# End of the second layer's attention: scores of a step ahead of its product with v, and the last FFN's first weights loaded into attention's weight tiles

## The chip, the cores and the metric

The kernel runs on one core of one Trainium2 chip. The time is that of one execution in device microseconds (us). A run repeats the execution; the median of three runs of the kernel before is 3238.61 us (3231.18 to 3245.23). One further execution was profiled: it took 3235.61 us, its instructions span 3233.8 us, and the granted TensorE clock was 0.990 of full speed on average.

The engines are called as the profile calls them: PE is TensorE (matmuls), PEld its weight loads, DVE is VectorE, ACT is ScalarE, POOL is GpSimd, SP issues DMAs.

## The reference

Two layers, each `x = x + attention(norm(x)) * silu(ffn(norm(x)))`, on x of 4 x 1024 x 512 in fp32. The change concerns the second layer, from the end of its attention on:

```python
# attention of layer 1: 16 heads of 32, rotary positions, softmax over 1024 keys
q, k, v = proj(wq), proj(wk), proj(wv)
q, k = apply_rope(q, k, sin, cos)
att = softmax(einsum('bhqd,bhkd->bhqk', q, k) / sqrt(32))
y = einsum('bhqk,bhkd->bhqd', att, v)
s = y.reshape(b, t, c) @ wo.T

# FFN of layer 1: weights are int32, DIM = 512, HID = 1408
def _qlinear(x, wq, scale):
    W = (wq.astype(float32) - 128.0) * scale[:, None]
    return einsum('bsd,hd->bsh', x, W)
g = silu(_qlinear(silu(_qlinear(x, wq_gate, s_gate)) * _qlinear(x, wq_up, s_up), wq_down, s_down))
x = x + s * g
```

## The kernel before

The kernel has four stages, one after the other: attention and FFN of layer 0 (to about 1200 us of the span), attention of layer 1 (1200 to 2714 us) and FFN of layer 1 (2714 us to the end). On PE the order of instructions is the order in which the program gives them. On the other engines and on SP's DMA queue a scheduler sets the order when the kernel is built, unless an instruction is kept in program order. Every queue is worked off strictly in its order. Tiles come from pools by a tag; a tag with `bufs` buffers hands them out in turn, and a new tile waits until the readers of the tile that had the buffer are done.

**Attention of layer 1** (L702 to L1018) works in 32 units: a batch, a group of four heads and a half of the 1024 queries each. Keys are cut into 8 blocks of 128. The main loop (L933) makes one step `s` after the other. In step `s` the unit's scores are first computed for their maxima alone (`top`, L863: PE into two PSUM tiles `sq`, DVE reduces each, L876). After 8 steps `turn_max` (L878) transposes the maxima; ACT copies them twice and DVE forms `mT` (L888). Ten steps behind (`LAG`), step `e = s - 10` computes its scores again, transposed, with the maxima subtracted by a second matmul (`expo`, L892: tiles `sk`, matmuls L899 and L905), and ACT takes the exponential of the two halves (L910) into `pT`, which has three buffers. `weigh` (L914) multiplies the `pT` of step `e - 1` with v into `y`. POOL sums the `pT` of a unit's 8 steps into `part` (L1013, L1015), and `total` (L809) sums `part` over the keys with a matmul by ones. For the last unit there is no `part`: PE sums each of its 8 `pT` (`z_last`). `divide` (L817) copies the sums (ACT), inverts them in four pieces (DVE, L825) and scales y (POOL, L826) to `yT`. `sq` and `sk` share three PSUM tiles (`ring`).

Within a step the order on PE is: `sq`, then `weigh` of `e - 1`, then a piece of other work (projections of the next heads, or the output projection `wo_out`, L829), then `expo` of `e`, then more of the other work. After step 255 there are no maxima left and, but for the sums, no other work: steps 256 to 266 only run `weigh` and `expo`. Then eight chains of the output projection follow, four for each half of the last batch's queries, each with an ACT copy and a DMA of its result.

**FFN of layer 1** (`ffn1_slots`, L1026) opens its pools when those of attention are closed. It loads 33 integer weight tiles (11 each of gate, up and down, 256 KB) through four staging buffers `wint`; DVE subtracts 128 (`weight`, L1050, L1058). The activations of a block of 512 tokens come in four pieces and are split into two parts, by ACT and DVE (`prep2`, L1032 to L1046). Per slot a gate and an up chain of eight matmuls each are made, and up to four pairs of matmuls for the down product of earlier slots (`down`, L1102). `gate` (L1112) makes the output of a tile of 128 tokens: DVE, ACT (L1121), DVE, DVE, POOL (L1124), DMA out, with two buffers for each of its four tiles. DVE also takes each weight tile's greatest magnitude (`most`, L1146), which decides at the end whether a second path has to run; the program places these from slot 22 on.

Of the kernel before, what the change touches and what calls it, by code (L numbers as in the profile page):

```python
# [12 lines left out]
F32 = mybir.dt.float32  # L13
# [22 lines left out]
def kernel(ctx, tc, ins, out):  # L36
# [634 lines left out]
    s1_t = s1.rearrange("(t p) d -> t p d", p=P)  # L671
    with ExitStack() as es:
# [3 lines left out]

        w0 = es.enter_context(tc.tile_pool(name="a1w", bufs=1, reuse_waits="tile"))
# [244 lines left out]

        es.enter_context(tc.manual_schedule(engines={mybir.EngineType.PE}))
# [9 lines left out]
        for s in range(TB * nu + LAG + 1):  # L933
# [27 lines left out]
            if s < TB * nu:  # L961
                u, j = divmod(s, TB)
                if j == 0:
                    mx[u] = p2.tile([P, TPB, 4, 2], F32, tag="mx", name=f"mx_{u}")
                for pair in range(2):
                    top(u, j, pair, mx[u])
                if j == TB - 1:
                    m2 = twice[u % 2].rearrange("p q (h c) -> p q h c", c=HD)
                    for c in range(2):
                        nc.vector.tensor_reduce(m2[:, :, :, c], mx[u], AX.X, ALU.max, negate=True)  # L970
                    del mx[u]
            if 1 <= e <= TB * nu:
                u, kb = divmod(e - 1, TB)
                if kb == 0:
                    ys[u] = pp.tile([P, 512], F32, tag="y", name=f"y_{u}")
                weigh(u, kb, pTs[e - 1], ys[u])
                if u == nu - 1:

                    if kb == 0:
                        z_last = acc1("z_last")  # L980
                    total(z_last, pTs[e - 1], kb, TB)
                pTs.pop(e - 2, None)
                if kb == TB - 1:
                    yr = p2.tile([P, 512], F32, tag="yr", name=f"yr_{u}", bufs=1)
                    nc.scalar.copy(yr, ys[u])
                    ys[u] = yr
                    if u == nu - 1:
                        divide(units[u], yr, z_last)
            held = 0
            if s % TB == 0 and 0 < s <= TB * nu:  # L990
                turn_max(s // TB - 1)
            elif s % TB == 4 and 0 <= s // TB - 2 < nu - 1:
                u = s // TB - 2
                z = ring(f"z_{u}")[:, 0, :] if s >= TB * nu else acc1(f"z_{u}")
                total(z, parts.pop(u), 0, 1)
                divide(units[u], ys.pop(u), z)
                b, g, qh = units[u]
                if g == 3:
                    soon[s + 4] = b, qh, yTs[b]
            elif s in lates:  # L1000
                late_turn(*lates.pop(s))
            else:
                held = 1
                advance(1)
            if 0 <= e < TB * nu:
                u, kb = divmod(e, TB)
                pT = pTs[e] = p2.tile([P, 4, 512], F32, tag="pT", name=f"pT_{e}", bufs=3)
                expo(u, kb, pT)
                if u == nu - 1:
                    pass  # L1010
                elif kb == 1:
                    parts[u] = p2.tile([P, 4, 512], F32, tag="part", name=f"part_{u}")
                    nc.gpsimd.tensor_tensor(parts[u], pTs[e - 1], pT, ALU.add)  # L1013
                elif kb:
                    nc.gpsimd.tensor_tensor(parts[u], parts[u], pT, ALU.add)  # L1015
            advance(4 - held)
        for new in [*soon.values(), (*units[-1][::2], yTs[B - 1])]:
            spare.extend(wo_out(*new, spread))  # L1018
        for chain in spare:
            advance(8)  # L1020
# [5 lines left out]
    def ffn1_slots():  # L1026
# [8 lines left out]
        def prep2(blk):  # L1035

            b, h = divmod(blk, 2)
            xs = p2.tile([P, KD, BLK], F32, tag="xs", name=f"xs_{blk}", bufs=1)
            xp = [a.bitcast(F32R) for a in xpair(f"xp1_{blk}")]
            for k in range(KD):  # L1040
                nc.sync.dma_start(out=xs[:, k, :], in_=xnT_d[b][k, :, h * BLK : (h + 1) * BLK])
                nc.scalar.copy(xp[0][:, k, :], xs[:, k, :])
                nc.vector.tensor_tensor(
                    xp[1][:, k, :], xs[:, k, :], xp[0][:, k, :].bitcast(F32), ALU.subtract
                )
            return xp  # L1046

        ws = {}

        def weight(n, c):  # L1050
            q = p2.tile([P, KD, P], I32, tag="wint", name=f"{n}_int{c}", bufs=4)
            if n == "down":
                src = ins["wq_downT"][c * P : (c + 1) * P, :].rearrange("p (k n) -> p k n", n=P)
            else:
                src = ins[f"wq_{n}T"][:, c * P : (c + 1) * P].rearrange("(k p) n -> p k n", p=P)
            nc.sync.dma_start(out=q, in_=src)
            w = ws[n, c] = wp.tile([P, KD, P], F32R, tag=f"{n}{c}", name=f"w{n}{c}")
            nc.vector.tensor_scalar(w, q, -128.0, None, ALU.add)  # L1058

        xp = prep2(0)  # L1060
        sg = wp.tile([P, NH1], F32, tag="sg", name="sg")
        nc.sync.dma_start(out=sg, in_=ins["s_gate"])
        su = wp.tile([P, NH1], F32, tag="su", name="su")
        nc.sync.dma_start(out=su, in_=ins["s_up"])
        for c in range(NH1 + 2):
            for n, d in (("gate", c), ("up", c), ("down", c - 2)):
                if 0 <= d < NH1:
                    weight(n, d)
        sdb = wp.tile([P, D], F32, tag="sdb", name="sdb")
        nc.sync.dma_start(out=sdb, in_=ins["s_down"].partition_broadcast(P))  # L1070

        sg2 = wp.tile([P, NH1], F32, tag="sg2", name="sg2")
        nc.vector.tensor_scalar(sg2, sg, 0.5, None, ALU.mult)
        sgu = wp.tile([P, NH1], F32, tag="sgu", name="sgu")
        nc.vector.tensor_tensor(sgu, sg2, su, ALU.mult)

# [35 lines left out]
        def gate(blk, i):  # L1112
            t = blk * TPB + i
            s = p2.tile([P, D], F32, tag="s", name=f"s1_{t}")
            nc.sync.dma_start(out=s, in_=s1_t[t])
            x = p2.tile([P, D], F32, tag="x", name=f"x2_{t}")
            nc.sync.dma_start(out=x, in_=x1_t[t])
            z = p2.tile([P, D], F32, tag="z", name=f"z1_{t}")
            nc.vector.tensor_tensor(z, ds.pop(i), sdb, ALU.mult)
            th = p2.tile([P, D], F32, tag="th", name=f"th1_{t}")  # L1120
            nc.scalar.activation(th, z, AF.Tanh, scale=0.5)  # L1121
            nc.vector.scalar_tensor_tensor(th, th, 1.0, z, ALU.add, ALU.mult)
            nc.vector.scalar_tensor_tensor(th, th, 0.5, s, ALU.mult, ALU.mult)  # L1123
            nc.gpsimd.tensor_tensor(th, th, x, ALU.add)  # L1124
            nc.sync.dma_start(out=out_t[t], in_=th)
# [3 lines left out]
        for g in range(NH1 * NBLK + 2 + 2 * TPB):  # L1129
            blk, c = divmod(g, NH1)  # L1130
            if blk < NBLK:
                gated(blk, c, xp)
                if c == 5 and blk + 1 < NBLK:
                    nxt = prep2(blk + 1)
# [10 lines left out]
            if 0 <= m < len(order):  # L1145
                nc.vector.tensor_reduce(  # L1146
                    most[:, m : m + 1], ws[order[m]].bitcast(F32), AX.XY, ALU.max,
                    apply_absolute_value=True,
# [118 lines left out]
    with ExitStack() as es1:  # L1267
# [78 lines left out]
```

## Time and profile before

| what | value |
|---|---|
| median of three runs | 3238.61 us |
| the profiled execution, its own time | 3235.61 us |
| its span, first to last instruction | 3233.8 us |
| PE busy in the span | 3116.0 us, 96% |
| DVE, ACT, POOL busy | 58%, 37%, 47% |
| share of PE in the chain that ended last | 80% |
| attention's last step with maxima has its scores | 2631.1 us |
| last matmul of the last output chain of attention | 2714.5 us |
| first matmul of the last FFN | 2723.2 us |
| last matmul of the last FFN | 3220.2 us |

PE is busy for 96% of the span on average, so time can be won only where it waits, and lost wherever it is made to wait. An average hides where that is: it is read from windows of 10 us and from the chain of waits, which follows the work that ended last back from instruction to instruction. A busy PE is also not always a fast one, because its clock is lowered at times; the windows show the granted clock beside the busy time.

### The profile page before, as it was taken

The numbers are of one execution on the slowest core, as the hardware profiler recorded it, in microseconds if no ns is written. First come the engines' busy times: TensorE is split into PE (matmuls) and PEld (weight loads), VectorE is DVE, ScalarE is ACT, GpSimd is POOL, SyncE is SP. The second block draws the span as 40 slices with busy tenths as digits, with TensorE's granted clock in tenths as the row PEclk, the third lists the DMA queues.
The fourth block names the chain that finished last, engine by engine and source line by source line (L and its number), as shares of the span: only waits on it lengthen the run. The fifth ranks groups of instructions, "written<-read, shape, count | busy, mean of one in ns | idle before, by whom it ended". The sixth has DMA issues, their size and how long they took to land.

```text
span 3233.8 us, 61080 instructions
## 1 busy us (share of the span) xinstructions
PE 3116.0 (96%) x26221; PEld 1764.0 (55%) x26221; DVE 1876.7 (58%) x2670; ACT 1195.7 (37%) x1692; POOL 1510.1 (47%) x618
## 2 busy tenths in 40 slices
PE   8999999999999998999999999999999988999998
PEld 4555455577777764343344444433444325788886
DVE  6434743368888775556655655555555643755554
ACT  2111111055556542444444444444444442233222
POOL 0000000024444343898888888888988860000001
PEclk9999999999999999999999999999999999999999
DMA  5100300022222231100001000100000004222212
GB/s 190 55 27 27 103 29 14 24 69 78 89 79 69 92 131 51 37 8 8 8 17 39 13 10 13 41 15 15 11 15 14 11 1 138 96 74 66 69 49 66
DMA packets 96503, 158.46 MB, mean 49 GB/s; under 512 B 12896, under 2 KB 26464, under 8 KB 96096
## 3 DMA queue, kind: packets, MB, share of 16 engines
q1 hardware_dynamic: 95408, 151.33, 14.9%
q8 instruction: 207, 3.39, 0.4%
q0 software_dynamic: 816, 3.15, 0.3%
q14 instruction: 72, 0.59, 0.1%
HBM read 104.10 MB, written 41.94 MB: 45 GB/s over the span
## 4 chain that ended last, share of the span: by engine, by line
PE 80%; DVE 11%; DMA 4%; ACT 2%; issue 2%; SPq 1%; POOL 0%; POOLq 0%; ACTq 0%; DVEq 0%
PE sk L899 9%; PE sq L872 8%; PE y L918 8%; PE qk L318 6%; PE dn L1107 5%; PE up L1085 5%; PE gate L1085 5%; PE v1ps L730 4%; PE pj L571 3%; PE fc L518 3%; PE wo L730 3%; PE wk L730 3%; PE wq L730 3%; PE v0ps L292 3%; PE wo L301 3%; PE sk L905 2%
## 5 line engine op out<-in xcount | busy, mean ns | idle before, releaser
L1015 POOL TENSOR_TENSOR part<-part,pT 128x2048 f32<-128x2048 f32 x186 | 854.3, 4593 | 19.7 <-ACT pT L910 10.3
L876 DVE TENSOR_REDUCE mx<-sq 128x2 f32<-128x1024 f32 x512 | 603.4, 1217 | 403.7 <-PE sq L872 402.5
L910 ACT ACTIVATE pT<-sk 128x1024 f32<-128x1024 f32 x512 | 496.4, 1022 | 631.2 <-PE sk L905 629.0
L899 PE MATMUL sk<-wqT,wkT 32*128 32x512 f32 x2048 | 327.5, 643 | 4.5 <-DVE mx L876 4.5
L872 PE MATMUL sq<-wkT,wqT 32*128 32x512 f32 x2048 | 323.6, 643 | 8.1 <-ACT pT L910 6.3
L918 PE MATMUL y<-pT,v 128*32 128x512 f32 x2048 | 284.4, 608 | 12.8 <-ACT pT L910 12.8
L571 PE MATMUL pj<-wpj,hp 128*128 128x512 f32 x1024 | 265.2, 397 | 16.6 <-DVE hp L531 16.2
L1124 POOL TENSOR_TENSOR th<-th,x 128x512 f32<-128x512 f32 x32 | 41.4, 1293 | 494.6 <-DVE th L1123 393.8
L539 POOL TENSOR_TENSOR sums<-sums,h 128x512 f32<-128x512 f32 x112 | 163.5, 1460 | 226.4 <-ACT h L523 223.4
L518 PE MATMUL fc<-xp,wfc 128*128 128x512 f32 x1024 | 262.2, 398 | 2.3 <-ACT h L523 1.7
L905 PE MATMUL sk<-mT,onesr 2*128 2x512 f32 x1024 | 237.1, 789 | 0.0
L318 PE MATMUL qk<-xnT,wqkv 128*128 128x512 f32 x512 | 231.7, 606 | 3.2 <-DVE s L306 2.4
L571 PEld LDWEIGHTS pj<-wpj,hp 128*128 128x128 f32 x1024 | 189.8, 188 | 69.4 <-DVE hp L531 27.7
L325 POOL TENSOR_TENSOR qd<-qT,wqkv 128x512 f32<-128x512 f32 x32 | 41.2, 1289 | 389.7 <-ACT qT L323 362.9
L518 PEld LDWEIGHTS fc<-xp,wfc 128*128 128x128 f32 x1024 | 188.7, 189 | 42.9 <-ACT h L523 3.3
L1085 PE MATMUL gate<-xp,wgate 128*128 128x512 f32 x704 | 180.1, 398 | 8.8 <-DVE wgate L1058 8.8
L1085 PE MATMUL up<-xp,wup 128*128 128x512 f32 x704 | 179.0, 396 | 1.6 <-DVE h L1092 1.6
L1013 POOL TENSOR_TENSOR part<-pT,pT 128x2048 f32<-128x2048 f32 x31 | 141.3, 4557 | 80.8 <-ACT pT L910 80.7
L1107 PE MATMUL dn<-wdown,hp 128*128 128x512 f32 x704 | 177.8, 394 | 0.0
L899 PEld LDWEIGHTS sk<-wqT,wkT 32*128 32x128 f32 x2048 | 97.3, 183 | 136.7 <-issue 114.6
L531 DVE TENSOR_TENSOR hp<-h,hp 128x512 fp32r<-128x512 f32 x128 | 119.9, 936 | 84.6 <-ACT hp L528 84.6
L918 PEld LDWEIGHTS y<-pT,v 128*32 128x32 f32 x2048 | 41.8, 108 | 216.4 <-issue 188.2
(203 smaller groups left out, 4570.2 us busy)
## 6 DMA issues: line engine op xcount, KB each, us to landing
s<-s SPq DMA_DIRECT2D x96, 256.0 KB
x<-x SPq DMA_DIRECT2D x36, 256.0 KB
x<-in_x SPq DMA_DIRECT2D x32, 256.0 KB
raw_fc<-in_w_fcT SPq DMA_DIRECT2D x32, 256.0 KB
raw_pj<-in_w_projT SPq DMA_DIRECT2D x32, 256.0 KB
x0f<-in_x SPq DMA_DIRECT2D x32, 256.0 KB
x0r<-in_x SPq DMA_DIRECT2D x32, 256.0 KB
x<-th SPq DMA_DIRECT2D x32, 256.0 KB
```

Source lines behind the costliest of these rows:

```text
L318: nc.tensor.matmul(a, lhsT=wqkv[k][:, c0 : c0 + P], rhs=xnTs[blk][:, k, :], start=(k == 0), stop=(k == KD - 1),)
L518: nc.tensor.matmul(a, lhsT=wfc[k][:, c * P : (c + 1) * P], rhs=xp[n][:, k, :].bitcast(F32R), start=(k == 0 and n == 0), stop=(k == KD - 1 ...
L571: nc.tensor.matmul(ds[i], lhsT=hparts[blk, c][n][:, i * P : (i + 1) * P], rhs=wpj[c], start=(c == 0 and n == 0), stop=(c == NH0 - 1 and n ...
L730: nc.tensor.matmul(out[r0 : r0 + HD, :], lhsT=lhsT[:, r0 : r0 + HD], rhs=rhs, start=start, stop=stop,)
L872: nc.tensor.matmul(sq[:, hh, :], lhsT=qT[r, q0 : q0 + P], rhs=kT[r, n * 512 : (n + 1) * 512], start=True, stop=True,)
L876: nc.vector.tensor_reduce(mx[:, qt, 2 * pair : 2 * pair + 2, n], sq, AX.X, ALU.max)
L899: nc.tensor.matmul(sks[h // 2][:, h % 2, :], lhsT=kT[r, kb * P : (kb + 1) * P], rhs=qT[r, qh * 512 : (qh + 1) * 512], start=True, stop=False,)
L910: nc.scalar.activation(pT[:, 2 * pair : 2 * pair + 2, :], sks[pair], AF.Exp, scale=QKS)
L918: nc.tensor.matmul(y[r, :], lhsT=v[:, kb, r], rhs=pT[:, h, :], start=(kb == 0), stop=(kb == TB - 1),)
L1015: nc.gpsimd.tensor_tensor(parts[u], parts[u], pT, ALU.add)
L1085: nc.tensor.matmul(a, lhsT=ws[n, c][:, k, :], rhs=xp[m][:, k, :], start=(k == 0 and m == 0), stop=(k == KD - 1 and m == 1),)
L1107: nc.tensor.matmul(ds[i], lhsT=hparts[blk, c][n][:, i * P : (i + 1) * P], rhs=w, start=(c == 0 and n == 0), stop=(c == NH1 - 1 and n == 1),)
```

## The change

It has five parts.

1. In steps 256 to 266 `expo` of step `e` goes ahead of `weigh` of step `e - 1` on PE. The sums of `pT` whose step lies there (`e` from 246 on) move from POOL to DVE. The last unit is summed by PE for its first four `pT` only; DVE adds the other four and PE sums the result, after the first four chains of the output projection. The sum of the last unit but one comes two steps later, and the last `divide` follows the last sum.
2. The first 16 of the last FFN's weight tiles are loaded in steps 240 to 255, one in each, through the two buffers of `raw`, and are converted by DVE one step later, into the tiles that held wk, wq, wv and the rotary table. These loads and conversions are kept in program order. The next four go into wo's tile, the rest into new tiles.
3. The first block's activations are loaded and split before the last four chains of the output projection (`parts1`), through `raw` as well. The other weights and activations go through six buffers `stage`.
4. The scales' small loads and products are made once, early in the program.
5. `gate` has four buffers instead of two for each of its tiles; for the last tile it works in two halves and its last addition is DVE's instead of POOL's. The magnitudes `most` are kept in program order.

```diff
+    sg, su, sg2, sgu = [
+        const.tile([P, NH1], F32, tag=n, name=n) for n in ("sg", "su", "sg2", "sgu")
+    ]
 ...
+    es1 = ExitStack()
+    w0 = es1.enter_context(tc.tile_pool(name="a1w", bufs=1, reuse_waits="tile"))
 ...
+    quads = ["wk", "wq", "wv", "cs", "wo"]
+    def weight(stage, pool, pinned=False):
+        m = len(ws)
+        n, c = needed[m]
+        q = stage(f"{n}_int{c}").bitcast(I32).rearrange("p (k n) -> p k n", n=P)
 ...
+        load = nc.sync.dma_start(out=q, in_=src)
+        j = m // 4
+        if j not in fours:
+            tag = quads[j] if j < len(quads) else f"wf{j}"
+            fours[j] = pool.tile([P, KD, D], F32, tag=tag, name=f"wf{j}")
+        w = ws[n, c] = fours[j][:, m % 4, :].bitcast(F32R).rearrange("p (k n) -> p k n", n=P)
+        if pinned:
+            tc.keep_in_program_order(load)
+        def less():
+            op = nc.vector.tensor_scalar(w, q, -128.0, None, ALU.add)
+            if pinned:
+                tc.keep_in_program_order(op)
+        return less
+    def parts1(blk, stage, pinned=False):
+        b, h = divmod(blk, 2)
+        xp = [a.bitcast(F32R) for a in xpair(f"xp1_{blk}")]
+        for k in range(KD):
+            xs = stage(f"xs_{blk}_{k}")
+            each = [
+                nc.sync.dma_start(out=xs, in_=xnT_d[b][k, :, h * BLK : (h + 1) * BLK]),
+                nc.scalar.copy(xp[0][:, k, :], xs),
+                nc.vector.tensor_tensor(
+                    xp[1][:, k, :], xs, xp[0][:, k, :].bitcast(F32), ALU.subtract
+                ),
+            ]
 ...
+        def exps(e):
+            if not 0 <= e < TB * nu:
+                return
+            u, kb = divmod(e, TB)
+            pT = pTs[e] = p2.tile([P, 4, 512], F32, tag="pT", name=f"pT_{e}", bufs=3)
+            expo(u, kb, pT)
+            k0 = TB // 2 if u == nu - 1 else 0
+            add = nc.vector if e + LAG >= TB * nu else nc.gpsimd
+            if kb == k0 + 1:
+                parts[u] = p2.tile([P, 4, 512], F32, tag="part", name=f"part_{u}")
+                add.tensor_tensor(parts[u], pTs[e - 1], pT, ALU.add)
+            elif kb > k0:
+                add.tensor_tensor(parts[u], parts[u], pT, ALU.add)
 ...
+            late_exp = s >= TB * nu
+            if late_exp:
+                exps(e)
             if 1 <= e <= TB * nu:
 ...
-                    total(z_last, pTs[e - 1], kb, TB)
+                    if kb < TB // 2:
+                        total(z_last, pTs[e - 1], kb, TB)
 ...
-                    if u == nu - 1:
-                        divide(units[u], yr, z_last)
 ...
+            zu = (s - (6 if s >= TB * nu else 4)) // TB - 2
 ...
-            if 0 <= e < TB * nu:
-                u, kb = divmod(e, TB)
-                pT = pTs[e] = p2.tile([P, 4, 512], F32, tag="pT", name=f"pT_{e}", bufs=3)
-                expo(u, kb, pT)
-                if u == nu - 1:
-                    pass
-                elif kb == 1:
 ...
+            if not late_exp:
+                exps(e)
             advance(4 - held)
-        for new in [*soon.values(), (*units[-1][::2], yTs[B - 1])]:
-            spare.extend(wo_out(*new, spread))
+            if s >= TB * (nu - 2) and s < TB * nu:
+                nxt = weight(raw1, w0, True)
+                if loaded:
+                    loaded()
+                loaded = nxt
+                if s == TB * nu - 1:
+                    loaded()
+        soon = [*soon.values()]
+        for new in soon:
+            spare.extend(wo_out(*new, lambda name: ring(name)[:, 0, :]))
         for chain in spare:
             advance(8)
+        total(z_last, parts.pop(nu - 1), TB - 1, TB)
+        divide(units[-1], ys.pop(nu - 1), z_last)
+        xp1 = parts1(0, raw1, True)
+        for chain in wo_out(*units[-1][::2], yTs[B - 1], spread):
+            advance(8)
 ...
-        xp = prep2(0)
 ...
+        xp = xp1
+        while len(ws) < len(needed):
+            weight(stage, w0 if len(ws) < 4 * len(quads) else wp)()
 ...
+            last = t == NTILE - 1
+            for h in range(2 if last else 1):
+                c = slice(h * D // 2, (h + 1) * D // 2) if last else slice(0, D)
+                nc.vector.tensor_tensor(z[:, c], d[:, c], sdb[:, c], ALU.mult)
+                nc.scalar.activation(th[:, c], z[:, c], AF.Tanh, scale=0.5)
 ...
+                (nc.vector if last else nc.gpsimd).tensor_tensor(th[:, c], th[:, c], x[:, c], ALU.add)
+                nc.sync.dma_start(out=out_t[t][:, c], in_=th[:, c])
```

## The prediction

> **What bounds the kernel now.** I read the page first: the chain that ended last is PE's for 80%, so a part of the change counts by what it does to PE's waits. The windows of 10 us then show where PE waits at the end of attention. Columns: busy time of PE, PEld, DVE, ACT and POOL, granted clock, DMA share, GB/s.
>
> ```profile
> 2590.00:2600.00 10.00, 9.15 (x48) 2.48 (x44) 7.60 (x5) 4.11 (x5) 9.77 (x3) 0.87 0.00 0
> 2600.00:2610.00 10.00, 10.00 (x48) 2.93 (x40) 3.19 (x3) 2.52 (x3) 2.92 (x1) 0.50 0.01 2
> 2650.00:2660.00 10.00, 7.68 (x56) 1.85 (x52) 3.39 (x4) 4.46 (x5) 0.67 (x1) 1.00 0.01 2
> 2710.00:2720.00 10.00, 4.45 (x76) 2.48 (x70) 0.13 (x1) 1.85 (x4) 0.00 (x0) 0.85 0.44 139
> 2720.00:2730.00 10.00, 6.76 (x22) 5.40 (x23) 8.88 (x19) 2.48 (x4) 0.00 (x0) 0.64 1.00 278
> 2740.00:2750.00 10.00, 10.00 (x43) 7.83 (x42) 9.14 (x19) 3.22 (x7) 0.00 (x0) 1.00 0.97 302
> ```
>
> Three places: half clock around 2600 to 2610 although PE looks busy, PE at 77% in the late steps, and the change of stage at 2710 to 2730, where DMA runs at 100% and the clock is low again. The chain of waits shows a late step:
>
> ```profile
> 2657.53 1.54 PE y L918 x6
> 2659.09 0.41 PE y L918 x2
> 2659.50 0.86 PE z_last L812 x6
> 2660.36 1.07 PE sk L899 x8
> 2661.43 0.28 PE sk L905 x3
> ...
> 2661.75 1.03 ACT pT L910
> ```
>
> It is serial: product, sum, scores, exponential, 5.3 us (the next product starts at 2662.83). The product takes 1.95 because its second half waits for ACT's second half; where both halves lie ready, the same chain has it at 1.00. The timelines of PE, POOL, DVE and ACT, and the rows of `mT` and of a conversion of layer 0, show the rest:
>
> ```profile
> 2723.24 3.75 PE L1085 MATMUL gate<-xp,wgate 128*128 128x512 f32 x8 [8.79 <-DVE wgate L1058]
> ```
> ```profile
> 2620.95 27.90 POOL L1015 TENSOR_TENSOR part<-part,pT 128x2048 f32<-128x2048 f32 x6
> ```
> ```profile
> 2636.08 3.77 DVE L888 SCALAR_TENSOR_TENSOR mT<-mh,second,mf 128x512 fp32r<-128x512 f32 x1 [5.74 <-ACT mh L886]
> 2687.56 3.39 DVE L825 RECIPROCAL zs<-zs 128x128 f32<-128x128 f32 x4 [28.37 <-ACT zs L821]
> ```
> ```profile
> L888 DVE SCALAR_TENSOR_TENSOR mT<-mh,second,mf x32: 739/2138/5015, 1266.2 to 2636.1; 128x512 fp32r<-128x512 f32 x32
> ```
> ```profile
> L178 DVE TENSOR_SCALAR neg_pj<-raw_pj,gam_pj x16: 455/486/1523, 382.1 to 676.0; 128x512 f32<-128x512 f32 x16
> ```
> ```profile
> 3224.86 0.63 ACT L1121 ACTIVATE th<-z 128x512 f32<-128x512 f32 x1 [3.81 <-DMA out<-th]
> ```
>
> PE waits 8.79 us for the FFN's first weights, then runs at half speed (3.75 us for eight matmuls that take 1.87 later). POOL's sums run back to back, 4.65 us each. `mT` takes 0.74 us alone and up to 5.02 us: it ends when the POOL addition running beside it ends. `neg`, a DVE operation with one SBUF input and a constant per partition, also goes from 0.49 to 1.52 us beside a POOL addition of layer 0. The last tile's tanh waits 3.81 us for an output DMA that holds its buffer.
>
> **Late steps (gain 19).** Before, from 2631.1 to the end of the last `z_last`, 2686.6: 55.5 us. After, PE's own work is 10 scores at 1.35 (1.07 + 0.28), 11 products at 1.00, four `z_last` and the other unit's sum at 0.86, one transposition at 0.6: 13.5 + 11 + 4.3 + 0.6 = 29.4 us; ACT's two exponentials (1.94 us a step) hide under it. About 0.6 is added at the start (the second scores tile needs the buffer that ACT reads until 2632.2) and 1.0 at the end. One wait is new: on DVE the addition for step 246 stands ahead of the last `mT`, and it needs POOL's addition for step 245, the fourth of the row above, which ends at 2620.95 + 4 x 4.6 = 2639.4. A DVE addition of 128x2048 took 2.28 us in layer 0 (L250), so `mT` is ready at 2639.4 + 2.3 + 0.7 = 2642.4. PE wants it at about 2638: 4.3 us. Behind `mT` on DVE waits the addition for 247, and ACT's third `pT` buffer with it; four reciprocals (3.39) stand ahead of the next additions. I add 1.2 for these: 36.5, a gain of 19. Bounds: 24 if POOL has no arrears, 2 if the buffers keep the steps at the 4.45 us that short steps before 2631 show (2621.84 to 2626.29).
>
> **Sixteen conversions in steps 240 to 255 (loss 5).** Each load has two steps, about 10 us, and a weight load lands in 4 to 4.6 us, so the DMA is hidden; SP's stores behind it have two `so` buffers of slack. The cost is on DVE. A conversion takes 0.42 us, but here POOL adds nearly all the time. If it waits for POOL as `mT` and `neg` do, DVE stands still, and behind it the maxima, whose buffers PE needs for the next scores. DVE is idle for 31.1 us in front of the 32 maxima of these 16 steps, 1.9 us a step, which absorbs part. Steps then lock to POOL: 4.55 + 0.07 + 0.42 = 5.04 us instead of the 4.1 to 4.6 us of about half of them, so 8 x 0.5 = 4; one or two collisions with `mT` or `yT` add 1 to 5, and POOL moved back by the conversions already counts in the arrears. I take 5. Below: 0. Above: a full addition less the idle time, 2.6 us, sixteen times: 42. The half clock at 2597 to 2611 lies in these steps and cost about 6 us (steps of 7.4 and 7.6 us beside 4.5 to 5.3). It follows a 3.62 us `mT`. I leave it in, since a conversion queued behind `mT` can wait as long; the gain if it goes is 6.
>
> The Trainium skill speaks against this part: "SBUF — State Buffer", section "Who interferes with whom", says that a DVE operation with two SBUF inputs, or in a mode with two ports, and a GpSimd operation exclude each other for a whole instruction, and counts tensor_scalar among those that can enter the mode. No run here shows the int32 conversion itself beside POOL; by the rule it waits, and the sum stays as it is below; if this form did not enter the mode, the sum would be 5 us better.
>
> **Output projection (loss 3.8).** The last sum, 0.86 us, now stands on PE between the two halves, and `divide` begins only then: ACT 0.59, DVE 3.39, POOL 1.28; before they ran from 2686.87 to 2692.37, 5.5 us, beside the first chains. After, the first of the last four chains has three quarters of 3.45 us that don't need it, 2.6. So 0.86 + 5.5 - 2.6 = 3.8. Activations for the FFN move into this stretch: four loads on SP, four ACT casts (0.62), four DVE subtractions (0.68), in two rounds of a DMA each, about 13 us of the 17.6 that PE has left; the stores of the last four chains wait behind the loads, with some 2 us to spare. If that cover went, a delay of the last copies would cost under 2.
>
> **Change of stage (gain 12.2).** From 2714.5 to the end of slot 8 at 2768.7 PE took 54.2 us for 176 matmuls (nine slots of 16, and down products of 2, 2, 4, 4, 6, 6 and 8 from the third slot on); at the later rate (1.865 for eight) they take 41.0, so 13.2 are lost. After, weights for six slots lie ready. The 17 others come at about 1 us each after a first DMA of 4 to 5 us, and slot 6 starts some 27 us in; but their conversions stand between the FFN's own work on DVE and each waits for its DMA, which can delay a gate tile's release: 0 to 2.5, I take 1.0.
>
> **Tail (gain 3.7).** Tanh starts at about 3221.0 instead of 3224.86, and POOL's 1.26 becomes a DVE half of 0.4, but both halves and the tile ahead queue on DVE, and POOL's addition for that tile can hold them up by 1.3: 2.5 to 4.8.
>
> **Small.** The scales' two DMA issues (0.38 + 0.43 on SP) and two DVE operations (0.17 + 0.16) move to the start: 0.4 lost, at most 1.1. `most` (0.68 each) moves from 2723 to 2770, where DVE is full, to slots with DVE idle: nothing, and covered by DVE's idle time of some 2 us a slot. Two new waits of PE, 4.3 and 2.9 us, may each bring a stretch of half clock (a wait of 2.4 us at 383 us was followed by one from 385.6 to 389.0 us, 3.4 us long, half of it lost): 1.7 for one.
>
> Sum: -19 + 5 + 3.8 - 12.2 - 3.7 + 0.4 + 1.7 = -24. From the profiled 3235.6 that is 3211.6; the median of the runs lies 3.0 higher, and I go halfway: 3213.
>
> **Rivals.** (A) Locks are cheap and the half clock goes: conversions 0, clock +6 and 1.7 not paid, 12.7 more: 3200. For it: the half clock is rare elsewhere in attention. Against: POOL is 98% busy at 2590. (B) The overlap does not come: three score buffers and three `pT` buffers keep the late steps at 4.45 us, so the part gains 2 and the whole 7 instead of 24: 3230. For it: the steps before 2631 with little other work run at that rate. Against: there the buffers are shared with the maxima, which are gone. (C) Slower: every conversion waits a whole POOL addition in front of the next maxima. Without conversions the change gains 29, so it decides from 1.8 us a conversion on; at 2.6 it is 42, 3249, and with the low clock kept longer more. For it: `mT` has done so at 5.02 us. Against: its median is 2.14, and after one wait DVE comes in step with POOL.
>
> **How the numbers follow.** My forecast 0.62, A 0.14, B 0.17, C 0.07. A measurement tells about 0.5% (16 us) from no change, so faster means under 3222. Of the forecast, whose own range is 3206 to 3222, 0.59 lies there, all of A and 0.01 of B: 0.74. Slower is 0.04 of C. The rest is 0.22. The range 3198 to 3232 takes in A and B with a little on either side and leaves out C and the edges, under 0.2 in all.
>
> **What would show it.** Right: conversions of 0.4 to 5 us on DVE ending with POOL's additions; late steps of 2.4 to 3.2 us; one wait of PE for `mT` near the first of them and one of about 3 us for `yT` in the output chains; no wait at the first gate. Wrong: late steps over 4 us (B), steps of 7 us in the stretch of the loads (C), or PE waiting for stage tiles in slots 3 to 6.

## The result, and the profile after

The changed kernel takes 3189.71 us (median of four runs, 3183.70 to 3195.80) against 3234.89 for the kernel before (3229.32 to 3245.23): a ratio of 0.9857, interval 0.9823 to 0.9890. It is 45 us faster. The forecast was 3213 with a range of 3198 to 3232: right in sign, with about half of the gain. The profiled execution of the changed kernel took 3183.70 us with a span of 3181.8 (before: 3235.61 and 3233.8).

Where the time went, between the same marks in both profiled executions:

| stretch | before, us | after, us | difference |
|---|---|---|---|
| start to the first scores of layer 1's attention | 1234.9 | 1230.4 | -4.5 |
| steps 0 to 239 | 1308.2 | 1306.6 | -1.5 |
| steps 240 to 254 | 83.25 | 79.62 | -3.6 |
| first score of step 255 to the last product with v | 59.7 | 43.3 | -16.4 |
| to the last matmul of the output projection | 28.5 | 32.0 | +3.5 |
| to the last down product of the FFN | 505.8 | 479.1 | -26.7 |
| to the end | 13.5 | 10.75 | -2.8 |
| span | 3233.8 | 3181.8 | -51.9 |

The windows of the changed kernel that answer to those shown of before (columns: busy time and instructions of PE, PEld, DVE, ACT, POOL; granted clock; DMA share; GB/s):

```profile
2590.00:2600.00 10.00, 9.86 (x68) 3.62 (x62) 10.00 (x8) 4.49 (x6) 7.11 (x2) 1.00 0.22 66
2640.00:2650.00 10.00, 10.00 (x94) 3.06 (x92) 0.00 (x0) 6.20 (x7) 0.00 (x0) 1.00 0.01 2
2690.00:2700.00 10.00, 10.00 (x76) 7.59 (x65) 4.31 (x8) 2.59 (x4) 0.00 (x0) 1.00 0.74 227
2700.00:2710.00 10.00, 10.00 (x46) 8.28 (x45) 9.11 (x21) 3.71 (x6) 0.00 (x0) 1.00 1.03 316
```

In the late steps (2640) PE is now busy all the time, at 94 matmuls where the kernel before had 56 in a window. At the change of stage (2690 to 2710) PE is never idle and the clock stays at 1.00, although the DMA is still at 74% to 103%: it loads weights that are needed later. In the stretch of the early loads (2590) DVE is at 100%; the window of before at the same place had 76%.

The chain of waits in a late step (start, length, what):

```profile
2643.43 1.07 PE sk L960 x8
2644.50 0.23 PE sk L966 x2
2644.72 1.00 PE y L979 x8
2645.72 0.86 PE z_last L873 x8
2646.58 1.07 PE sk L960 x8
```

A step is 3.15 us with the sum and 2.3 to 2.5 without, and no piece of ACT is left in it. The exponential runs beside the product of the step before it.

The two new waits of PE, and the first gate chain, from PE's timeline (start, length, line, tiles, shapes; in brackets the wait ahead of it and what ended it):

```profile
2634.03 0.51 PE L966 MATMUL sk<-mT,onesr 2*128 2x512 f32 x4 [2.07 <-DVE mT L949]
...
2680.55 1.72 PE L791 MATMUL wo<-wo,yT 128*32 128x256 f32 x28 [3.33 <-POOL yT L887]
```
```profile
2691.91 2.11 PE L1141 MATMUL gate<-xp,wf 128*128 128x512 f32 x8
```

The waits for `mT` and `yT` are there, and the 8.79 us in front of the first gate are gone. All this is as forecast. What was not is in the same view some 150 us later. Ahead are three chains of the kernel before, then three of the changed kernel; only the starts matter:

```profile
2886.20 2.03 PE L1085 MATMUL gate<-xp,wgate 128*128 128x512 f32 x8
2888.07 2.03 PE L1085 MATMUL up<-xp,wup 128*128 128x512 f32 x8
2889.93 2.02 PE L1107 MATMUL dn<-wdown,hp 128*128 128x512 f32 x8
2891.80 1.56 PE L1085 MATMUL gate<-xp,wgate 128*128 128x512 f32 x6
```
```profile
2846.19 1.98 PE L1141 MATMUL gate<-xp,wf 128*128 128x512 f32 x8
2848.01 1.98 PE L1141 MATMUL up<-xp,wf 128*128 128x512 f32 x8
2849.82 1.98 PE L1163 MATMUL dn<-wf,hp 128*128 128x512 f32 x8
2851.63 0.62 PE L1141 MATMUL gate<-xp,wf 128*128 128x512 f32 x2
```

24 matmuls with no wait between them take 5.60 us before and 5.44 after: 233 ns each against 227, at a granted clock of 1.00 in both. They are the same matmuls in the same order. The slot length stays at these values from the ninth slot to the end (but for some 0.1 us near the 58th slot in both). From the start of the tenth slot to the last down product it is 451.5 us before and 439.1 after, 12.3 us less. I had not forecast it, and it is more than half of the 21 us by which the forecast fell short.

### The profile page after: what moved, and what is told of

The parts are those of the page before. It is cut to its first block, busy times and chain, and to the rows that moved or that the text cites. A ratio compares the mean times of both kernels' runs of the same rounds, so it can differ in the third digit from the quotient of the medians.

```text
span 3181.8 us, 61073 instructions
## 1 busy us (share of the span) xinstructions
PE 3089.1 (97%) x26197; PEld 1763.2 (55%) x26197; DVE 1906.8 (60%) x2680; ACT 1196.0 (38%) x1693; POOL 1501.6 (47%) x615
## 3 DMA queue, kind: packets, MB, share of 16 engines
q0 software_dynamic: 816, 3.15, 0.3%
## 4 chain that ended last, share of the span: by engine, by line
PE 81%; DVE 12%; DMA 3%; ACT 2%; issue 1%; SPq 1%; POOL 1%; ACTq 0%; POOLq 0%; DVEq 0%
PE sk L960 9%; PE sq L933 8%; PE y L979 8%; PE qk L318 6%; PE gate L1141 5%; PE up L1141 5%; PE dn L1163 5%; PE fc L518 4%; PE pj L571 4%; PE v1ps L791 4%; PE wq L791 3%; PE wk L791 3%; PE wo L791 3%; PE v0ps L292 3%; PE wo L301 3%; PE sk L966 2%
## 5 line engine op out<-in xcount | busy, mean ns | idle before, releaser
L1000 POOL TENSOR_TENSOR part<-part,pT 128x2048 f32<-128x2048 f32 x184 | 844.6, 4590 | 23.0 <-ACT pT L971 13.9
L979 PE MATMUL y<-pT,v 128*32 128x512 f32 x2048 | 275.4, 608 | 0.2 <-ACT pT L971 0.2
L1141 PE MATMUL gate<-xp,wf 128*128 128x512 f32 x704 | 174.1, 389 | 0.0
L1141 PE MATMUL up<-xp,wf 128*128 128x512 f32 x704 | 173.9, 389 | 0.0
L1163 PE MATMUL dn<-wf,hp 128*128 128x512 f32 x704 | 173.5, 389 | 0.0
L318 PEld LDWEIGHTS qk<-xnT,wqkv 128*128 128x128 f32 x512 | 95.2, 191 | 115.9 <-issue 103.5
```

What stands on the lines that cost most here:

```text
L318: nc.tensor.matmul(a, lhsT=wqkv[k][:, c0 : c0 + P], rhs=xnTs[blk][:, k, :], start=(k == 0), stop=(k == KD - 1),)
L979: nc.tensor.matmul(y[r, :], lhsT=v[:, kb, r], rhs=pT[:, h, :], start=(kb == 0), stop=(kb == TB - 1),)
L1000: add.tensor_tensor(parts[u], parts[u], pT, ALU.add)
L1141: nc.tensor.matmul(a, lhsT=ws[n, c][:, k, :], rhs=xp[m][:, k, :], start=(k == 0 and m == 0), stop=(k == KD - 1 and m == 1),)
L1163: nc.tensor.matmul(ds[i], lhsT=hparts[blk, c][n][:, i * P : (i + 1) * P], rhs=w, start=(c == 0 and n == 0), stop=(c == NH1 - 1 and n == 1),)
```

## The experiments

All were timed beside the kernel before, on the same chip in each series; its medians in the three series were 3235.1, 3237.0 and 3235.0 us.

### What sets the pace of the FFN's matmuls

Two theories. *State*: after a wait PE falls into one of two rhythms and stays in it; the kernel before waits several times at the change of stage, the changed kernel does not. In the kernel before the distances from start to start alternate between 229 or 230 and 234 to 238 ns without end, which looks like such a rhythm. *Place*: the change moves tiles (the scales leave the pool in which they lay ahead of the weights), and the pace depends on where the operands lie in SBUF. In the built programs the operands' places differ modulo 512 bytes.

**Extra matmuls in the kernel before** disturb PE's rhythm without moving a tile.

```diff
+                cols = nudges.get((n, blk * NH1 + c), 0)
+                if cols:
+                    nc.tensor.matmul(a[:, :cols], lhsT=ws[n, c][:, 0, :],
+                                     rhs=xp[0][:, 0, :cols], start=True, stop=True)
```

> The kernel before with nine extra matmuls in the FFN, one ahead of the gate chain of slots 16, 24, 32 and so on to 80, of 128, 128, 256, 256, 384, 384, 512, 512 and 128 columns; the first matmul of the chain then overwrites what they wrote. They cost about 1 us in all. Theory of a state: after some of them the pace of the matmuls changes from 233.4 to 226.7 ns and stays so until the next one, up to 14 us gained. Theory of the place: the pace is 233.4 between all of them, and the kernel is 1 us slower than before.

Measured: 3239.84 us (ratio 1.0011, 0.9990 to 1.0031). Between all nine the slots stay at 5.59 us. That speaks against the state theory; the kernels with padding decide.

**A tile of padding ahead of the weights**, then one ahead of the other tiles too, both in the kernel before:

```diff
         nc.sync.dma_start(out=su, in_=ins["s_up"])
+        wp.tile([P, 480], F32, tag="pad", name="pad")
...
+        p2.tile([P, 96], F32, tag="pad2", name="pad2", bufs=1)   # second kernel only
```

> The kernel before with one edit: an unused tile of 1920 bytes ahead of the FFN's weight tiles, so that they lie at the same place modulo 2048 bytes as the activations, as in the changed kernel. Theory of the place: the FFN's matmuls come every 226.7 ns instead of 233.4, a slot takes 5.44 us instead of 5.59, and the whole is about 13 us faster than before. Theory of a state that PE falls into after a wait: nothing in the order of PE changes, so they stay at 233.4 and the time within 5 us of before.

> The kernel before with two unused tiles: 1920 bytes ahead of the FFN's weight tiles and 384 bytes ahead of the FFN's other tiles. Then the two operands of every FFN matmul start at the same place modulo 512 bytes, in the gate and up chains and in the down products too. If the place of the operands sets the pace, the down products come every 226.7 ns as well (they came every 232.6 with the first tile alone, and gate 226.7), a slot takes 5.44 us, and the whole is about 13 us faster than the kernel before. If the first tile helped by chance or for another reason, the down products stay at 230 to 233 and a slot at 5.49 or more.

And the reverse, **128 bytes of padding in the changed kernel**:

```diff
+        p2.tile([P, 32], F32, tag="pad2", name="pad2", bufs=1)
         def stage(name):
```

> The changed kernel with one unused tile of 128 bytes ahead of the FFN's stage, h and hp tiles, so that the operands of a down product no longer start at the same place modulo 512 bytes; those of gate and up still do. If the place of the operands sets the pace, only the down products slow down, from 226.7 to about 232.6 ns, a slot takes 5.49 us, and the whole is about 4.5 us slower than the changed kernel. If not, all stay at 226.7.

PE's timeline in the steady part of the FFN: one tile of padding, then two, then the changed kernel shifted.

```profile
2883.40 1.98 PE L1086 MATMUL up<-xp,wup 128*128 128x512 f32 x8
2885.22 2.02 PE L1108 MATMUL dn<-wdown,hp 128*128 128x512 f32 x8
2887.08 1.98 PE L1086 MATMUL gate<-xp,wgate 128*128 128x512 f32 x8
```
```profile
2883.13 1.98 PE L1088 MATMUL up<-xp,wup 128*128 128x512 f32 x8
2884.94 1.98 PE L1110 MATMUL dn<-wdown,hp 128*128 128x512 f32 x8
2886.76 1.98 PE L1088 MATMUL gate<-xp,wgate 128*128 128x512 f32 x8
```
```profile
2882.29 1.98 PE L1143 MATMUL up<-xp,wf 128*128 128x512 f32 x8
2884.11 2.02 PE L1165 MATMUL dn<-wf,hp 128*128 128x512 f32 x8
2885.97 1.98 PE L1143 MATMUL gate<-xp,wf 128*128 128x512 f32 x8
```

In the first, the up chain takes 1.82 us to the next start and the down products 1.86; in the second both take 1.81 to 1.82; in the third the down products alone are slow again. Over slots 24 to 57 of each profile, with the places from the built programs:

| kernel | xp, gate and up weights, hp, modulo 512 | gate, ns | down, ns | slot, us |
|---|---|---|---|---|
| before | 352, 480, 96 | 232.9 | 232.9 | 5.59 |
| one tile of padding | 352, 352, 480 | 226.7 | 232.6 | 5.49 |
| two tiles | 352, 352, 352 | 226.6 | 226.7 | 5.44 |
| changed | 96, 96, 96 | 226.6 | 226.7 | 5.44 |
| changed, shifted | 96, 96, 224 | 226.7 | 232.6 | 5.49 |

(Gate and up read xp and their weights; a down product reads hp and a weight tile that lies like the gate's.) The first tile alone gave a slot of 5.49 us and not the 5.44 expected, because hp still lay 128 bytes from the down weights. From the start of the tenth slot to the last down product it is 451.5 us before, 443.6 with one tile and in the shifted kernel, and 439.1 with two tiles and in the changed kernel. The pace is 226.7 ns where both operands start at the same place modulo 512 bytes and about 232.7 where they lie 128 bytes apart, whichever of the two was moved. In time: one tile 3229.05 us (0.9987, 0.9967 to 1.0008, which alone can't be told from no change), two tiles 3225.11 (0.9960, 0.9942 to 0.9978; 11.9 us faster than the kernel before beside it, 7 to 19 by the interval), the changed kernel shifted 3199.07 against 3189.71 and 3192.02 unshifted; the FFN alone, from the last output matmul to the last down product, is 484.0 us there against 479.1. So the place is the cause, and an edit that computes nothing is worth about 12 us here. Why the place matters isn't shown. In this FFN only equal places and distances of 128 bytes were compared, and whether a smaller modulus than 512 would describe them as well stays open.

### The change of stage and the conversions

**No early weights**: the block in steps 240 to 255 taken out, all 33 weights loaded when the FFN opens.

```diff
-            if s >= TB * (nu - 2) and s < TB * nu:
-                nxt = weight(raw1, w0, True)
...
```

> The changed kernel without the 16 loads and conversions in steps 240 to 255: all 33 weight tiles are loaded when the FFN opens, through the six stage buffers. Steps 240 to 255 show the price of a conversion: my forecast was 5 us for all, so they would take 5 us less than the 79.6 us of the changed kernel; if the conversions are free, within 1 us of it (both but for half clock, 1.7 us a stretch). At the change of stage PE waits for the first weights again, 8 to 9 us, and loses some 4 more: about 12 us slower there. The matmuls of the FFN's later slots tell a theory apart: if their pace (226.7 ns against 233.4 before) comes from where the weight tiles lie, they stay at 226.7, since the tiles lie as in the changed kernel; if it is a state that PE falls into after a wait, this kernel may show 233, since it waits as the kernel before does.

**No early activations**: the first block's activations loaded when the FFN opens.

```diff
-        xp1 = parts1(0, raw1, True)
...
-        xp = xp1
+        xp = parts1(0, stage)
```

> The changed kernel, but the first block's activations are loaded and split when the FFN opens, as before, and not ahead of the last output chains; the 16 weights are still loaded early. If the early activations carry their part of the gain at the change of stage, PE waits 6 to 9 us for them at the first gate and perhaps runs 3 to 7 us at half clock after it: 8 to 12 us slower than the changed kernel. If the weights alone were what PE waited for, under 2 us slower.

PE's timeline at the first gate, without the early weights and without the early activations:

```profile
2697.73 2.50 PE L1133 MATMUL gate<-xp,wf 128*128 128x512 f32 x5 [5.05 <-DVE wf L711]
```
```profile
2701.44 2.80 PE L1140 MATMUL gate<-xp,wf 128*128 128x512 f32 x5 [5.85 <-ACT xp L725]
```

Either one missing makes PE wait 5 to 6 us and lose some 2.5 more at half clock in the first slot. The FFN stretch grows from 479.1 us to 486.9 and 487.6, by 7.8 and 8.4; with neither (the kernel before with two tiles of padding) it is 495.3, by 16.2, which is the sum of the two, although that kernel also differs in its staging buffers and in the scales' loads. In time: 3193.90 (0.9880, 0.9846 to 0.9914) and 3195.81 (0.9876, 0.9855 to 0.9897). By the medians that is only some 4 us slower than the changed kernel in each case, and the intervals overlap with its own, so the prices rest on the profiles. The pace stayed at 226.7 ns in both, although PE waits, which speaks once more against the state theory.

The first of the two also shows what the conversions cost. Steps 240 to 254 take 77.2 us without them and 79.6 in the changed kernel, neither with half clock: 2.4 us, and fourteen of the sixteen conversions lie in them. (The expectations call this stretch 240 to 255.) DVE's timeline of the changed kernel shows why they cost anything:

```profile
2569.88 3.72 DVE L711 TENSOR_SCALAR wf<-gate_int 128x512 fp32r<-128x512 int32 x1
2573.53 2.34 DVE L937 TENSOR_REDUCE mx<-sq 128x2 f32<-128x1024 f32 x2
2575.79 2.46 DVE L711 TENSOR_SCALAR wf<-up_int 128x512 fp32r<-128x512 int32 x1
...
2587.80 0.41 DVE L711 TENSOR_SCALAR wf<-gate_int 128x512 fp32r<-128x512 int32 x1
```

Ten of the sixteen take 0.85 to 3.72 us instead of 0.36 to 0.42, and each of these ten ends 0.28 us after the POOL addition that ran beside it. "SBUF — State Buffer" of the Trainium skill, section "Who interferes with whom", counts tensor_scalar among the operations that can exclude a GpSimd operation for a whole instruction; the prediction said that no run showed it for this form, and this one does.

### The late steps

Steps 256 to 266 as before: product first, sums on POOL, the last unit summed on PE.

```diff
-            add = nc.vector if e + LAG >= TB * nu else nc.gpsimd
+            add = nc.gpsimd
...
-            late_exp = s >= TB * nu
+            late_exp = False
...
-                    if kb < TB // 2:
-                        total(z_last, pTs[e - 1], kb, TB)
+                    total(z_last, pTs[e - 1], kb, TB)
```

> The changed kernel, but steps 256 to 266 as in the kernel before: product ahead of the next scores, sums on POOL, the last unit summed by PE alone. If the overlap of exponential and product is the gain that I predicted, the time from the scores of step 255 to the last product goes back from 43.3 us to about 59.7, the last output chains no longer wait 3.3 us for yT, and the whole is about 13 us slower than the changed kernel. If the gain in those steps came from something else (other clock, loads off the queue), they stay near 43 us and the whole within 5 us.

Its chain of waits:

```profile
2651.56 0.86 PE z_last L873 x6
2652.42 1.07 PE sk L960 x8
2653.49 0.28 PE sk L966 x3
2653.77 0.04 issue
2653.81 1.03 ACT pT L971
```

ACT is back in the chain and a step takes 5.29 us. From the first score of step 255 to the last product it is 59.9 us against 43.3, and from there to the end of the output projection 28.5 against 32.0, without the wait for `yT`. The two together, 13.1 us, are what this part is worth, half clock included (none in this profile, 10.2 us in these steps of the changed kernel's). In time it is 3201.66 us (0.9900, 0.9867 to 0.9933), 12.0 more than the 3189.71 of the changed kernel.

### The tail

```diff
-            s = p2.tile([P, D], F32, tag="s", name=f"s1_{t}", bufs=4)
+            s = p2.tile([P, D], F32, tag="s", name=f"s1_{t}")
...
-            last = t == NTILE - 1
+            last = False
```

> The changed kernel with the tail of the kernel before: two buffers for each tile of the output stage, and the last tile in one piece, its last addition on POOL. My forecast for the tail was a gain of 3.7 us, bounds 2.5 to 4.8: so the time from the last down product to the end is 10.75 us in the changed kernel and 13.3 to 15.6 here. Rival: the tail's gain came with the rest, and it stays within 1 us of 10.75.

3193.64 us (0.9857, 0.9827 to 0.9887). From the last down product to the end it is 13.0 us, against 10.4 to 10.8 in all kernels with the new tail: 2.2 to 2.6 us. Before, the last tile's tanh waited 3.81 us for an output DMA, and here it waits 2.68; in the changed kernel the last tanhs wait only for DVE, and one operation of the second half (1.48 us, where the first half's took 0.42) ends 0.28 us after POOL's addition:

```profile
3171.05 1.31 ACT L1182 ACTIVATE th<-z 128x512 f32<-128x512 f32 x3 [2.14 <-DVE z L1181]
3173.55 1.32 POOL L1185 TENSOR_TENSOR th<-th,x 128x512 f32<-128x512 f32 x1 [1.78 <-DVE th L1184]
3173.68 1.48 DVE L1183 SCALAR_TENSOR_TENSOR th<-th,z 128x256 f32<-128x256 f32 x1
```

In time alone, with 3189.7 and 3192.0 for the changed kernel, it could not be told from nothing.

### Versions

> The changed kernel once more, without an edit, as the measure for the others of this series. The stages that the profile shows should repeat: a slot of 5.44 us, a wait of about 2.1 us for mT and 3.3 us for yT, 10.5 to 11 us from the last down product to the end. What does not repeat is chance: the start of layer 0 (its FFN ended at 1179.6 us in the first profile and at up to 1187.7 in kernels that differ from it later only) and the half clock around steps 247 and 256.

3192.02 us (0.9861, 0.9842 to 0.9880): the difference to before is 43 us here and 45 in the first series. The slot and the `yT` wait (3.34) repeat. The `mT` wait does not appear in this profile: half clock from 2631.9 us on slowed PE there, so that `mT` was ready.

**Two moves**: the last sum and division behind the first output chain, and the last `mT` ahead of the addition for step 246.

```diff
-        for chain in spare:
+        for n, chain in enumerate(spare):
             advance(8)
-        total(z_last, parts.pop(nu - 1), TB - 1, TB)
-        divide(units[-1], ys.pop(nu - 1), z_last)
+            if n == 0:
+                total(z_last, parts.pop(nu - 1), TB - 1, TB)
+                divide(units[-1], ys.pop(nu - 1), z_last)
...
+            if e + LAG == TB * nu:
+                turn_max(nu - 1)      # ahead of the addition, both kept in program order
```

> The changed kernel with two moves. The last unit's sum and division go behind the first of the four output chains instead of the fourth; DVE's last addition ended at 2662.5 us in the changed kernel and that chain at 2662.4, so PE should wait at most 1 us there, and the wait of 3.3 us for yT should go. And the last mT goes ahead of the addition for step 246 on DVE, so that the wait of 2.1 us for it should go. If both waits are real losses, the whole is about 5 us faster than the changed kernel, with perhaps 1.7 to 3.4 more if the half clock in the late steps goes; if they only move to another place, the time is as in the changed kernel.

3183.14 us (0.9830, 0.9805 to 0.9855; the changed kernel had 0.9857 and 0.9861, with intervals that overlap this one). Both waits are gone; no wait of PE over 0.5 us is left between step 255 and the end of the FFN, and the output projection is back at 28.5 us instead of 32.0. Its profile has 13.65 us of half clock in the late steps all the same, so that half clock doesn't come from those two waits.

**With the early conversions on ACT**, and, apart from that, **with padding in layer 0**:

```diff
-            op = nc.vector.tensor_scalar(w, q, -128.0, None, ALU.add)
+            if pinned:
+                op = nc.scalar.activation(w, q, AF.Identity, bias=m128)
```
```diff
+        p2.tile([P, 80], F32, tag="pad0", name="pad0", bufs=1)
         for c in range(wpj0, NH0):
```

> The kernel with the two moves (sum and division behind the first output chain, mT ahead of the addition), and with the 16 early conversions on ACT instead of DVE, which waits for POOL's additions there. If that wait is what the conversions cost, steps 240 to 255 fall from 79.6 us (without half clock) to about 77.2, the value without conversions, and the whole is 2.4 us faster than with the two moves alone. If ACT, which takes the exponentials, delays them by its conversion of about 0.6 us a step, the steps gain nothing or lose up to 5 us.

> The kernel with the two moves, and with an unused tile of 320 bytes ahead of the tiles of layer 0's FFN, so that there too both operands of each matmul start at the same place modulo 512 bytes; for 640 of its 1024 projection matmuls (of two instructions each in 320 cases) they did not. If the place sets the pace there as in layer 1, those come every 226.7 ns instead of about 231, and layer 0 is 2 to 4 us shorter. If the pace of 227 to 236 ns in layer 0 is an after-effect of PE's many short waits there (0.09 us in front of most chains), nothing changes.

On ACT: 3180.91 us (3180.50 to 3182.51; 0.9832, 0.9816 to 0.9848), the lowest median here, 11 us under the changed kernel of the same series, but not to be told from the two moves alone (3183.14, 0.9830). Each conversion takes 0.72 to 0.74 us:

```profile
2557.88 0.72 ACT L714 ACTIVATE wf<-up_int,m 128x512 fp32r<-128x512 int32 x1
```

Its steps 240 to 254 took 83.0 us, because 13.65 us of half clock fell into them; the thirteen others are within 0.04 us of those without loads and conversions. So the early loads and ACT's conversions cost these steps nothing, and the 2.4 us are the conversions on DVE. The 2.4 us expected for the whole can't be read from the time. Padding in layer 0: 3182.25 us (0.9829, 0.9809 to 0.9849), which can't be told from the two moves alone. There the distance from one projection matmul to the next fell from 231 to 228.3 ns, but layer 0's FFN, which takes 487.6 to 487.8 us from its second block on in the thirteen other profiles, took 486.66: 1.1 us and not the 2 to 4 expected. From 760 to 1180 us PE waits 14.1 us for `hp` there, and 14.2 with the padding, so the wait is not what took the rest; the chains that follow a wait still run at 224 to 236 ns a matmul for a while, with the padding too. (The words "two instructions each in 320 cases" in that expectation are a slip: it is 640 matmul instructions.)

## Why the prediction was right and wrong

**Late steps (forecast -19, and 1.7 for half clock).** Right. The last `z_last` ended at 2686.8 us before, 60.5 us after the first score of step 255; the last product now ends 43.3 after it: -17.2, half clock included (10.2 us of it in these steps after, none before). Undone alone: -16.6 to the last product and -0.9 for the sum moved behind it, -17.5. The wait for `mT` had the right cause and was 2.1 us instead of 4.3, because half clock (6.8 us from 2617.3 on) made PE late for it; in the kernel without the early weights, with no half clock ahead of it, it was 3.59. Rival B is out: three score buffers and three `pT` buffers let a step run in 2.3 to 3.15 us.

**Conversions (forecast +5).** Right mechanism, sized too high: they wait for POOL's additions as said, but DVE's idle time took up more: +2.4. The steps did not lock to POOL as the sum had it, 0.5 us in each of eight: four of them, 245, 246, 253 and 254, lost 3.6 us together, and step 249 became 1.2 shorter. Rival C, which needed 1.8 us lost for each conversion, is far off: 0.17.

**The half clock that was left in.** The changed kernel's profile has none at steps 250 and 251, 5.9 us less than before (14.9 against 9.0 in the kernel without the early weights). But it isn't won. The four kernels with the old attention have 6.8 to 20.5 us of it, starting at 2596 to 2599 us; of the eight profiles with conversions on DVE, none has it there, but five have 3.4 to 6.8 us at step 247, and seven have some between 2617 and 2640. Rival A was half right for the profiled execution (the conversions cost 2.4 and not 0, and the late steps had 10.2 us of half clock), and it can't be counted on.

**Output projection (forecast +3.8).** Right: +4.4 in the forecast's own count (0.9 for the sum and 3.3 of waiting), +3.5 from the last product.

**Change of stage (forecast -12.2).** Right in what happens: no wait at the first gate, six slots' weights ready, no stage tile ever late. In the forecast's own stretch, to the end of slot 8, the 54.3 us became 40.0: -14.3 instead of -12.2. The difference is the 1.0 that the forecast added for late gates, which didn't come, and 1.1 of the pace. The other 12.3 of the 26.7 us are the pace of the later slots. The forecast took both early loads as one; left out alone, the weights cost 7.8 and the activations 8.4, so each is worth about half of the stage's gain.

**The pace (forecast: none).** This is the step that failed. The working said "at the later rate (1.865 for eight)", took that rate from the trace of before for the kernel after, and never asked whether it could move, since the matmuls were the same. It moved by 2.7% because tiles moved. In the sum, everything behind slot 8 stood at nothing; it was 12.3 us, more than the 8 us by which the time lies under the range: with it the forecast's -24 becomes about -36. The stage, the conversions and the tail were off by less, 0.9 to 2.6 us each.

**Tail (forecast -3.7, bounds 2.5 to 4.8).** -2.8 by the profiles, 2.2 to 2.6 undone alone: at the low bound. As the forecast said, the halves queue on DVE and one is held up by POOL, by 1.07 us.

**Small (forecast +0.4).** Not seen. Layer 0 began its FFN 4.5 us earlier in the first profile, but in fourteen profiles that begin varies from 650.7 to 661.9 us whatever the kernel, and the changed kernel's second profile has the latest: chance of the start, not the change.

The sum of what was measured, -17.2 + 2.4 + 4.4 - 26.7 - 2.8, is -40; with 5.9 of half clock and 6.0 of chance ahead of step 240 it is the -51.9 of the two profiled executions. The medians say -45 and -43; the 3 to 5 us between these and -40 are not assigned to a part.

## What to carry to other kernels

Where a change moves tiles, compare their addresses in the built programs before taking any matmul's pace from the old trace: the same chain ran 2.7% slower because its two operands lay 128 bytes apart modulo 512, and two unused tiles repaired it, one for each kind of chain. Work that is only waiting at a change of stage is worth loading early in full, since leaving out either half brings back half of the loss. And an operation to be put on DVE beside long POOL additions is worth a trial on ACT: there the conversions cost the steps nothing, though the whole time didn't show the difference.

## What the runs showed of the hardware

- The pace of back-to-back 128x128x512 matmuls with a weight load each was 226.7 ns or about 232.7 ns by the place of their operands, at a granted clock of 1.00. "SBUF — State Buffer" of the Trainium skill, section "Who interferes with whom", gives PE two read ports, one for the moving operand and one for weight loads, and calls them independent; the runs show that the two operands' places are not indifferent to each other, and don't show what it is that they share.
- The slow pace alternates from one matmul to the next (229 or 230 and 234 to 238 ns) and doesn't settle; after nine deliberate disturbances it came back each time.
- An int32 to fp32r TENSOR_SCALAR on DVE that started while POOL added 128x2048 was held until that addition ended: ten of ten ended 0.28 us after it (changed kernel). The same conversion on ACT took 0.72 to 0.74 us beside the same additions.
- Half clock near the end of attention changes its place and length between kernels whose work there is the same. The kernel before and its three versions with padding or extra matmuls, which differ from it only later, have 6.8 to 20.5 us of it in steps 250 to 252, and the changed kernel, profiled twice, has 10.2 and 23.9 us of it from step 247 to the end of the output projection. What decides it stays open.
